# Unpacking 4-bit weights without the exclusive or, and a reordered opening, in a macaron block on one core

## The chip, the cores and the metric

The kernel runs on one NeuronCore of a Trainium2 chip. Its engines work side by side, each in the order of its own queue: TensorE (PE) multiplies and transposes into PSUM, VectorE (DVE) and ScalarE (ACT) work on SBUF and PSUM, GpSimd (POOL) on SBUF only, and SyncE (SP) starts most transfers. ACT and POOL start a few transfers too. Semaphores carry the waits between engines. The metric is the device time of one execution in microseconds (us), as the median of several runs.

## The reference

The input `u` has 2 x 1024 rows of 1024 values (2048 tokens). Three blocks are added to it in turn:

```python
x = x + 0.5 * ffn(layernorm(x))
x = x + s4(layernorm(x))          # a convolution along the last axis, by FFT, plus D * u
x = x + 0.5 * ffn(layernorm(x))

# ffn, with weights packed as 4-bit numbers, eight in a 32-bit word:
W[k, n] = scales[k // 128, n] * (w4[k, n] - (z4[k // 128, n] + 1))
h = silu(x @ Wg) * (x @ Wu)       # 1024 -> 2752
out = h @ Wd                      # 2752 -> 1024
```

Both feed-forward blocks use the same weights. `z4` are zero points, packed in the same way, one for each group of 128 rows.

## The kernel before

**Jobs.** The tokens are cut into four blocks of 512. Each block passes twice through the feed-forward part, so there are eight jobs (`JOBS`), and `fast()` writes them out one after the other. A job has a gate/up stage (`gate_up`, L650) and a down stage (`down`, L713). The gate/up stage has 48 steps: seven waves of column tiles (`WAVES`), each with eight groups of 128 input rows. A wave of three column tiles has six units (gate and up), held in six PSUM banks. In each step every unit gets two matmuls of 128x128 by 128x512, one with the low part and one with the high part of the activations. Then the unit's accumulator is multiplied by the ratio of two groups' scales: even units on ACT (L620), odd ones on DVE (L622). The next step's matmul on this bank waits for that. The down stage has 2 x 22 steps of four accumulators, in the same manner. The S4 block of a token block is worked in between the steps of the following job.

**Weights.** Nothing is stored unpacked at the start. In job 0 the packed words are loaded (`fetch`, L445), the zero points are loaded from a table in DRAM (`fetch_zeros`, L452, from `z_dram`, which `zero_points` writes at L305), and `signed_bytes` unpacks: a shift and mask for the even numbers (L459), one for the odd (L461), an addition of the zero-point table (L465), and an exclusive or with 0x8080 that turns biased bytes into signed ones (L467). All four are on DVE. `dequantize` (L499) copies every fourth byte of a row into a dense int8 tile `q` (pool of four buffers), on POOL, and SP writes it to DRAM (L503). From there each step's tile of int8 weights is loaded (`load_bytes`, L580, four steps ahead) and cast to fp32r three steps ahead (`make_weights`, L594 to L598): on POOL, but on ACT for three of eight steps in job 0. The down weights are unpacked in the same way (`dequantize_down`, L531), late in job 0's gate/up stage and during its down stage. All later jobs load the int8 weights.

**Order.** `at(hooks, s, f)` puts a piece of work ahead of step `s`. Engines' queues are filled by a planner that simulates the instructions with a cost of its own and takes, on each engine, the earliest written instruction that is ready in this simulation. `in_order_of_writing(f, engines)` binds what `f` writes to the written order on these engines, behind what was written before; what is written later is not bound to it.

**Opening.** `start()` (L1434) loads the packed zero points on ACT's queue, the rows of the first 512 tokens on SP's and ACT's, then packed words and scales. DVE unpacks the zero points, writes them to `z_dram`, and takes the moments of four row tiles (L186). Wave 0 is unpacked with zero points read back from `z_dram`. DVE and POOL share wave 0's eight byte copies; its first tile also goes directly from `q` into SBUF (L502, on POOL's queue), and DVE casts it (L594). ACT subtracts means (L1422), multiplies by inverse deviations (L1426), PE transposes, and ACT and DVE copy the result in two parts into `xT` (L246, L247). The second half of the columns follows in steps 0 to 3 (`second_half`).

Of the kernel before, what the change touches and what calls it, by code (L numbers as in the profile page):

```python
# [9 lines left out]
F32 = mybir.dt.float32  # L10
BF16 = mybir.dt.bfloat16
F16 = mybir.dt.float16
I32 = mybir.dt.int32
I8 = mybir.dt.int8
U16 = mybir.dt.uint16
F32R = mybir.dt.float32r
AF = mybir.ActivationFunctionType
# [6 lines left out]
P = 128  # L24
# [30 lines left out]
def macaron_s4_kernel(  # L55
# [116 lines left out]
    def rows_of(dram, b):  # L172
        return [dram[bass.ds(b * TB + t * P, P), :] for t in range(NT)]

    def moments(b, k, then=None):
        for _ in moments_by_tile(b, k, then):
            pass

    def moments_by_tile(b, k, then=None):

        name = f"{b}_{k}"
        stats = small.tile([P, NT, 2, 6], F32, tag="stats", name=f"stats_{name}")
        mv = small.tile([P, NT, 2], F32, tag="mv", name=f"mv_{name}")
        for t in range(NT):
            for i in range(2):
                nc.vector.bn_stats(stats[:, t, i, :], x[b][t][:, bass.ts(i, 512)])  # L186
            nc.vector.bn_aggr(mv[:, t, :], stats[:, t, :, :].rearrange("p a s -> p (a s)"))
            if then:
                then(t, mv[:, t, 0:1])
            yield  # L190
        ve = small.tile([P, NT], F32, tag="ve", name=f"ve_{name}")
        nc.vector.tensor_scalar(ve, mv[:, :, 1], EPS, None, ALU.add)
        r = small.tile([P, NT], F32, tag="r", name=f"r_{name}")
        half = small.tile([P, NT], I32, tag="half", name=f"half_{name}")
        nc.vector.tensor_scalar(half, ve.bitcast(I32), 1, None, ALU.logical_shift_right)
        nc.vector.tensor_scalar(
            r.bitcast(I32), half, -1.0, float(0x5F3759DF), ALU.mult, ALU.add
        )
        ln[b] = (mv, ve, r)
# [79 lines left out]
            nc.scalar.dma_start(z[own], src.rearrange("g (s n) -> (g s) n", s=SEG))  # L279
        return z  # L280

    def zero_points(which, z):

        p, n = z.shape
        zi = t2(f"zi_{which}").bitcast(I32)[:p, : 8 * n]
# [9 lines left out]
        tab = t2(f"ztab_{which}").bitcast(I32)[:p, : 8 * n]  # L295
        nc.vector.tensor_scalar(
            tab.bitcast(U16).rearrange("p (n k) -> p n k", k=2),
            zi.unsqueeze(2).to_broadcast([p, 8 * n, 2]),
            -8.0 * 257,
            120.0 * 257,  # L300
            ALU.mult,
            ALU.add,
        )
        dst, seg, queue = (zd_dram, SEGD, nc.sync) if which else (z_dram, SEG, nc.scalar)
        queue.dma_start(dst.rearrange("g (s n) -> (g s) n", s=seg), tab)  # L305

# [128 lines left out]


    first_tile = bpool.tile([P, width_of(0)], I8, tag="b", name="b_0_0")
    packed = {}
    NIBBLES = 0x78787878

# [14 lines left out]
    def signed_bytes(key, raw, even, z):  # L455

        nc.vector.tensor_scalar(even, raw, 3, NIBBLES, ALU.logical_shift_left, ALU.bitwise_and)  # L459
        yield  # L460
        nc.vector.tensor_scalar(raw, raw, 1, NIBBLES, ALU.logical_shift_right, ALU.bitwise_and)  # L461
        yield
        for part in (even, raw):
            both = part.bitcast(U16)
            nc.vector.tensor_tensor(both, both, z.bitcast(U16), ALU.add)  # L465
            yield
            nc.vector.tensor_scalar(both, both, 0x8080, None, ALU.bitwise_xor)  # L467
            yield
        view = lambda a: a.bitcast(I8).rearrange("p (n k) -> p k n", k=4)
        packed[key] = view(even), view(raw)  # L470

    def split(w):
        raw, z = packed[w]
        even = t4(f"even_{w}").bitcast(I32)[:, : width_of(w)]
        return signed_bytes(w, raw, even, z)

    def in_pieces(at, hooks_and_steps, pieces):

# [16 lines left out]
    def dequantize(w, j):  # L495

        q = qpool.tile([P, width_of(w)], I8, tag="q", name=f"q_{w}_{j}")
        engine = nc.vector if w == 0 and j % 3 < 2 else nc.gpsimd
        engine.tensor_copy(q, packed[w][j % 2][:, j // 2, :])  # L499
        dst = w_q[w].rearrange("(r j) n -> j r n", j=8)[j]  # L500
        if w == 0:
            nc.gpsimd.dma_start(first_tile[j:P:8], q[: P // 8])  # L502
        nc.sync.dma_start(dst, q)  # L503
        if j == 7:
            packed.pop(w)

# [15 lines left out]

    def split_down(a, rt):
        both, z = packed[a, rt]
        return signed_bytes((a, rt), both[:, 0], both[:, 1], z)

    def dequantize_down(a, rt, j):
        src = packed[a, rt][j % 2][:, j // 2, :]
        n = src.shape[0]
        q = qpool.tile([P, 512], I8, tag="q", name=f"qd_{a}_{rt}_{j}")[:n]  # L530
        nc.gpsimd.tensor_copy(q, src)  # L531
        rows = wd_q[a][8 * P * rt : 8 * P * rt + 8 * n]
        nc.sync.dma_start(rows.rearrange("(r j) n -> j r n", j=8)[j], q)
        if j == 7:
            packed.pop((a, rt))

    def first_weights(up, dn, at):


        for w in range(1, len(WAVES)):  # L540
            s0 = 8 * w - 12
            if w > 1:
                both = lambda w=w: (fetch(w), fetch_zeros(w))
                at(up, max(0, s0 - 5), lambda both=both: in_order_of_writing(both, ET.SP))
                steps = [(up, max(1, s0 - d)) for d in (3, 2, 2, 1, 1, 1)]
                in_pieces(at, steps, lambda w=w: split(w))
            else:
                both = lambda: [None for _ in split(1)]
                at(up, 0, lambda both=both: in_order_of_writing(both, *STARTING))
            for j in range(8):  # L550
                s = s0 + j if w > 1 else j // 2
                at(up, s, lambda w=w, j=j: dequantize(w, j))
        s0 = len(STEPS) - 12
        when = lambda n: (up, s0 + n) if n < 12 else (dn, (5 * (n - 12)) // 6)
        for n in range(6 * 8):
            k, j = divmod(n, 8)
            a, rt = divmod(k, 3)
            if j == 0:
                at(*when(max(0, n - 7)), lambda a=a, rt=rt: fetch_down(a, rt))
                steps = [when(max(0, n - d)) for d in (4, 3, 3, 2, 1, 0)]  # L560
                in_pieces(at, steps, lambda a=a, rt=rt: split_down(a, rt))
            at(*when(n), lambda a=a, rt=rt, j=j: dequantize_down(a, rt, j))

# [25 lines left out]
    def make_weights(i):  # L589
        j, stage, s = queue[i]  # L590
        b = loaded.pop(i)
        made[i] = t = wpool.tile(list(b.shape), F32R, tag="w", name=f"w_{stage}_{j}_{s}")
        if i == 0:
            nc.vector.tensor_copy(t, b)  # L594
        elif j == 0 and stage == "up" and s % GK in (1, 2, 5):
            nc.scalar.copy(t, b)
        else:
            nc.gpsimd.tensor_copy(t, b)  # L598
# [710 lines left out]
    def fast():  # L1309
        for j, (b, k) in enumerate(JOBS):  # L1310
# [50 lines left out]
            if j == 0:  # L1361
                rows = {3: srow_next}
                for s, k0, k1 in ((4, 3, 9), (16, 9, 15), (32, 15, WIDE)):
# [2 lines left out]
                        at(up, s - 5, load)  # L1366
                    at(up, s - 2, lambda k0=k0, k1=k1: scales(k0, k1, rows.pop(k0)))
                at(up, 40, scales_down)
                for t in range(NT):
                    at(up, t, lambda t=t: in_order_of_writing(lambda: second_half(t), *STARTING))  # L1370
                first_weights(up, dn, at)
# [59 lines left out]

    means = {}

    def start():  # L1434
        zeros = zero_words(0)
        x[0] = [t4(f"x_0_{t}") for t in range(NT)]
        for t, src in enumerate(rows_of(u, 0)):
            (nc.sync, nc.scalar)[t // 2].dma_start(x[0][t], src)
        fetch(0)
        srow = scale_rows(0, 3)  # L1440
        zeros_down = zero_words(1)
        fetch(1)
        rows_next = scale_rows(3, 9)
        zero_points(0, zeros)
        fetch_zeros(0)
        fetch_zeros(1)

        def then(t, m):
            means[t] = m
            less_mean(t, 0)  # L1450
            if t == 2:
                next(first_bytes)
                next(first_bytes)

        first_bytes = split(0)
        moments(0, 1, then)
        deviations(0, 1, -LIFT)
        for _ in first_bytes:
# [12 lines left out]
        return rows_next  # L1471

    srow_next = in_order_of_writing(start, *STARTING)
    x.pop(0)
    fast()
    x.clear()
# [85 lines left out]
```

## Time and profile before

| | |
|---|---|
| median of three runs | 2150.17 us (2148.67 to 2150.4) |
| profiled execution | 2152.6 us, of which the span 2150.7 |
| PE / DVE / ACT / POOL busy | 2092.5 / 1704.3 / 1422.3 / 1062.5 us |
| first gate/up matmul | 29.04 us |
| DMA, mean | 62 GB/s |

The profile is one execution on the chip. Busy time of an engine is the time in which at least one of its instructions ran; the ends of matmuls are modelled, so a busy PE isn't PE at its peak, and counting matmuls says more. A group's row gives line, engine, operation, result and operands, how many, and then busy time, mean ns of one, and the idle time just before with what ended it. The chain of waits is followed back from the last instruction, each time to what released it.

### The profile page before, as it was taken

How to read it: one execution, taken by the hardware profiler on the slowest of the kernel's cores; microseconds unless marked ns; L12 is line 12 of the kernel's file. 1: busy time of each engine (PE TensorE's matmuls, PEld its weight loads, DVE VectorE, ACT ScalarE, POOL GpSimd, SP SyncE). 2: the span in 40 equal slices, each digit the busy share in tenths (PEclk: the TensorE clock that was granted, in tenths of full speed). 3: DMA queues.
4: the chain of work that ended last, by engine and by line, in shares of the span. 5: the costliest groups of instructions: out<-in, count | busy, mean ns of one | idle time of the engine just before them, and what ended most of it. 6: DMA issues, size and time to landing. Idle time of an engine off the chain costs nothing.

```text
span 2150.7 us, 30258 instructions
## 1 busy us (share of the span) xinstructions
PE 2092.5 (97%) x9748; PEld 1425.5 (66%) x9748; DVE 1704.3 (79%) x2783; ACT 1422.3 (66%) x2233; POOL 1062.5 (49%) x1420
## 2 busy tenths in 40 slices
PE   4999999999999999999999999999999999999998
PEld 2555675577867568665776568676686766866576
DVE  7888978578788877778777788878788787777776
ACT  5887677646654776676767767646776467767765
POOL 3767747554344543455335553454534455345642
PEclk9999999999999999999999999999999999999999
DMA  4425232112111211212221121112111121121111
GB/s 136 116 85 148 78 92 59 32 54 76 41 41 54 89 53 39 78 33 58 87 80 36 31 74 37 38 52 77 35 36 41 52 93 48 44 81 36 34 35 57
DMA packets 163544, 132.49 MB, mean 62 GB/s; under 512 B 22252, under 2 KB 151029, under 8 KB 163376
## 3 DMA queue, kind: packets, MB, share of 16 engines
q1 hardware_dynamic: 162528, 129.12, 19.9%
q8 instruction: 79, 1.29, 0.3%
q10 hardware_dynamic: 592, 1.25, 0.2%
q14 instruction: 89, 0.73, 0.1%
q0 software_dynamic: 256, 0.10, 0.0%
HBM read 104.79 MB, written 25.50 MB: 61 GB/s over the span
## 4 chain that ended last, share of the span: by engine, by line
PE 87%; DVE 7%; POOL 2%; issue 1%; DMA 1%; ACT 1%; SPq 0%; DVEq 0%; ACTq 0%; POOLq 0%
PE pg L650 53%; PE po L713 27%; PE pc L1040 3%; DVE pg L622 2%; PE pb L735 1%; PE pb L1040 1%; PE pt L224 1%; DVE po L622 1%; PE st L224 1%; POOL w_down L598 0%; DVE hf L680 0%; POOL qd L531 0%; PE s_k L954 0%; DVE even L465 0%; ACT g L677 0%
## 5 line engine op out<-in xcount | busy, mean ns | idle before, releaser
L620 ACT ACTIVATE pg<-pg,rat 128x512 f32<-128x512 f32 x1240 | 787.3, 661 | 435.7 <-PE pg L650 434.8
L622 DVE TENSOR_TENSOR pg<-pg,rat 128x512 f32<-128x512 f32 x1168 | 776.1, 693 | 182.4 <-PE pg L650 178.4
L650 PE MATMUL pg<-xTh,w_up 128*128 128x512 f32 x2752 | 852.3, 438 | 6.3 <-DVE pg L622 4.5
L650 PE MATMUL pg<-xTl,w_up 128*128 128x512 f16 x2752 | 723.2, 383 | 13.6 <-DVE w_up L594 6.6
L650 PEld LDWEIGHTS pg<-xTh,w_up 128*128 128x128 f32 x2752 | 520.2, 189 | 185.2 <-DVE pg L622 18.3
L598 POOL CAST w_up<-b 128x768 fp32r<-128x768 int8 (+2 forms) x487 | 377.6, 781 | 529.6 <-PE pg L650 428.6
L713 PE MATMUL po<-hl,w_down 128*128 128x512 f32 x1344 | 538.8, 403 | 9.4 <-DVE po L622 7.3
L620 ACT ACTIVATE po<-po,ratd 128x512 f32<-128x512 f32 x660 | 431.0, 662 | 158.9 <-PE po L713 158.7
L713 PE MATMUL po<-hh,w_down 128*128 128x512 f32 x1344 | 522.4, 391 | 0.0
L622 DVE TENSOR_TENSOR po<-po,ratd 128x512 f32<-128x512 f32 x620 | 427.0, 697 | 96.6 <-PE po L713 92.6
L650 PEld LDWEIGHTS <-w_up 128*128 128x128 bf16 x2752 | 228.4, 99 | 335.3 <-issue 153.1
L598 POOL CAST w_down<-bd 128x512 fp32r<-128x512 int8 x352 | 222.5, 634 | 405.3 <-PE po L713 340.7
L713 PEld LDWEIGHTS po<-hl,w_down 128*128 128x128 f32 x1344 | 251.9, 188 | 86.2 <-DVE po L622 20.5
L713 PEld LDWEIGHTS po<-hh,w_down 128*128 128x128 f32 x1344 | 252.8, 188 | 45.2
L684 POOL TENSOR_TENSOR hl<-hf,hh 128x512 fp32r<-128x512 f32 x168 | 217.0, 1292 | 7.9
L680 DVE SCALAR_TENSOR_TENSOR hf<-pg,rat,g 128x512 f32<-128x512 f32 x168 | 122.9, 748 | 47.0 <-ACT g L677 37.4
L677 ACT ACTIVATE g<-pg,rat 128x512 f32<-128x512 f32 x168 | 110.6, 687 | 48.8 <-PE pg L650 38.9
L682 POOL CAST hh<-hf 128x512 fp32r<-128x512 f32 x168 | 106.4, 633 | 62.6 <-PE pg L650 30.5
L186 DVE BATCH_NORM_STATS2 stats<-x 128x6 f32<-128x512 f32 x96 | 63.6, 676 | 0.5
L1070 DVE TENSOR_TENSOR x<-x,pc 128x512 f32<-128x512 f32 x32 | 21.9, 685 | 36.9 <-PE pc L1040 36.9
L224 PE MATMUL pt<-ident,xn 128*128 128x128 f32 x256 | 43.2, 282 | 7.7 <-ACT xn L1426 7.7
L1040 PEld LDWEIGHTS pc<-near,st 128*128 128x128 f32 x256 | 43.6, 190 | 7.9
(177 smaller groups left out, 1043.3 us busy)
## 6 DMA issues: line engine op xcount, KB each, us to landing
b<-wq SPq DMA_DIRECT2D x319, 96.0 KB
bd<-wdq SPq DMA_DIRECT2D x336, 64.0 KB
x<-in_L_attn_u_dram SPq DMA_DIRECT2D x30, 512.0 KB
b<-wq SPq DMA_DIRECT2D x128, 64.0 KB
xs<-x SPq DMA_DIRECT2D x16, 512.0 KB
x<-xs SPq DMA_DIRECT2D x16, 512.0 KB
out_dram<-x SPq DMA_DIRECT2D x16, 512.0 KB
b<-wq SPq DMA_DIRECT2D x64, 80.0 KB
```

What stands on the lines that cost most here:

```text
L186: nc.vector.bn_stats(stats[:, t, i, :], x[b][t][:, bass.ts(i, 512)])
L224: nc.tensor.transpose(ps[:, bass.ts(k, P)], n[:, bass.ts(k, P)], ident)
L598: nc.gpsimd.tensor_copy(t, b)
L620: nc.scalar.activation(dst, src, AF.Copy, scale=sc)
L622: nc.vector.tensor_tensor(dst, src, sc.to_broadcast([P, TB]), ALU.mult)
L650: nc.tensor.matmul(p, weights, (lo, hi)[k][:, g, :], start=(g == 0 and not done), stop=(g == GK - 1 and done), skip_group_check=True,)
L677: nc.scalar.activation(g, pg, AF.Silu, scale=rat[:, 2 * f, GK - 1 :])
L680: nc.vector.scalar_tensor_tensor(hf, pu, last, g, ALU.mult, ALU.mult)
L682: nc.gpsimd.tensor_copy(hi, hf)
L684: nc.gpsimd.tensor_tensor(lo, hf, hi.bitcast(F32), ALU.subtract)
L713: nc.tensor.matmul(ps[c], w[:, bass.ts(c, P)], part, start=(f == 0 and k == 0), stop=(f == NF - 1), skip_group_check=True,)
L1040: nc.tensor.matmul(dst, lhsT, rhs, start=start, stop=stop, skip_group_check=True)
```

## The change

There are three parts.

- Unpacking leaves the bytes biased by 128 (`biased_bytes`): the exclusive or is gone, two of six DVE operations for each wave and each piece of the down weights. The byte copy now subtracts 128 from an unsigned byte (`to_signed`), on POOL, for two tiles of wave 0 on ACT. Since there are fewer operations, the pieces are placed otherwise: a wave's four operations come together one step ahead of its first copies, a down piece's four in four successive places; a wave is fetched three steps ahead instead of five.
- In the opening, the packed words of wave 0 and its packed zero points come first, the rows after them. The zero points of wave 0 are spread over their rows by the load itself (`first_zero_words`) and unpacked in place (`first_zeros`), so wave 0 no longer reads `z_dram`. DVE unpacks and POOL and ACT copy bytes before the moments are taken. ACT takes the moments of row tile 1 (a mean by accumulation, then squares of the differences), DVE those of the other three. `zero_points(0)` comes at the end of the opening, that of the down weights at step 12, and the second halves' mean subtractions (for three tiles) after `zero_points(0)`. The first tile's transfers move from POOL's queue to SP's. The first three casts are on POOL. An activation with Silu at the start loads ACT's table.
- `keep_warm` gives PE transposes whose result nobody reads: 12 before the first turn, one after each turn, six after the last. PE, too, is now bound to the written order in the opening.

The diff (without the renaming of callers and the import of `U8`):

```diff
@@ def moments_by_tile(b, k):
             nc.vector.bn_aggr(mv[:, t, :], stats[:, t, :, :].rearrange("p a s -> p (a s)"))
-            if then:
-                then(t, mv[:, t, 0:1])
             yield
+        guess(b, k, mv)
+
+    def guess(b, k, mv):
...
+    def unpacked_zeros(tab, z, zi):
...
+    def zero_points(which, z):
+        p, n = z.shape
+        zi, tab = (t2(f"{a}_{which}").bitcast(I32)[:p, : 8 * n] for a in ("zi", "ztab"))
+        unpacked_zeros(tab, z, zi)
         dst, seg, queue = (zd_dram, SEGD, nc.sync) if which else (z_dram, SEG, nc.scalar)
...
+    def first_zero_words():
+        n = width_of(0) // 8
+        z = t2("zq_first").bitcast(I32)[:, :n]
+        for own, i, lo, hi in columns(0):
+            own = slice(own.start // 8, own.stop // 8)
+            src = (gate_qz, up_qz)[i][:, lo // 8 : hi // 8]
+            wide = src.unsqueeze(1).to_broadcast([GK, 16, own.stop - own.start])
+            nc.scalar.dma_start(z[:, own], wide)
+        return z
+
+    def first_zeros(zq):
+        n = width_of(0)
+        z, zi = (t4(f"{a}_w0").bitcast(I32)[:, :n] for a in ("z", "zi"))
+        unpacked_zeros(z, zq, zi)
+        packed[0][1] = z
...
             nc.vector.tensor_tensor(both, both, z.bitcast(U16), ALU.add)
             yield
-            nc.vector.tensor_scalar(both, both, 0x8080, None, ALU.bitwise_xor)
-            yield
-        view = lambda a: a.bitcast(I8).rearrange("p (n k) -> p k n", k=4)
+        view = lambda a: a.bitcast(U8).rearrange("p (n k) -> p k n", k=4)
...
+    def to_signed(q, part, on_act=False):
+        if on_act:
+            nc.scalar.activation(q, part, AF.Identity, bias=minus_128)
+        else:
+            nc.gpsimd.tensor_scalar(q, part, -128.0, None, ALU.add)
...
-        engine = nc.vector if w == 0 and j % 3 < 2 else nc.gpsimd
-        engine.tensor_copy(q, packed[w][j % 2][:, j // 2, :])
+        to_signed(q, packed[w][j % 2][:, j // 2, :], on_act=w == 0 and j in (0, 2))
         if w == 0:
-            nc.gpsimd.dma_start(first_tile[j:P:8], q[: P // 8])
+            nc.sync.dma_start(first_tile[j:P:8], q[: P // 8])
...
-                at(up, max(0, s0 - 5), lambda both=both: in_order_of_writing(both, ET.SP))
-                steps = [(up, max(1, s0 - d)) for d in (3, 2, 2, 1, 1, 1)]
-                in_pieces(at, steps, lambda w=w: split(w))
+                at(up, s0 - 3, lambda both=both: in_order_of_writing(both, ET.SP))
+                in_pieces(at, [(up, s0 - 1)], lambda w=w: split(w))
...
-                steps = [when(max(0, n - d)) for d in (4, 3, 3, 2, 1, 0)]
+                steps = [when(max(0, n - d)) for d in (3, 2, 1, 0)]
...
-        if i == 0:
-            nc.vector.tensor_copy(t, b)
-        elif j == 0 and stage == "up" and s % GK in (1, 2, 5):
+        if j == 0 and stage == "up" and s > 2 and s % GK in (1, 2, 5):
             nc.scalar.copy(t, b)
...
+                zeros = lambda: zero_points(1, zeros_down)
+                at(up, 12, lambda: in_order_of_writing(zeros, ET.DVE, ET.SP))
...
+    def first_moments():
+        stats = small.tile([P, NT, 2, 6], F32, tag="stats", name="stats_0_1")
+        mv = small.tile([P, NT, 2], F32, tag="mv", name="mv_0_1")
+        own = 1
+        means.update({t: mv[:, t, 0:1] for t in range(NT)})
+        scratch = t4("scratch")
+        nc.scalar.activation(
+            scratch, x[0][own], AF.Copy, scale=1.0 / HID, accum_out=means[own]
+        )
+        for half in range(2):
+            less_mean(own, half)
+        squares = small.tile([P, 2], F32, tag="squares", name="squares")
+        for half in range(2):
+            nc.scalar.activation(
+                scratch[:, bass.ts(half, 512)], first[own, half], AF.Square,
+                scale=HID**-0.5, accum_out=squares[:, half : half + 1],
+            )
+        for t in (0, 2, 3):
+            for i in range(2):
+                nc.vector.bn_stats(stats[:, t, i, :], x[0][t][:, bass.ts(i, 512)])
+            nc.vector.bn_aggr(mv[:, t, :], stats[:, t, :, :].rearrange("p a s -> p (a s)"))
+            less_mean(t, 0)
+        nc.vector.tensor_tensor(mv[:, own, 1:2], squares[:, 0:1], squares[:, 1:2], ALU.add)
+        guess(0, 1, mv)
+
+    def keep_warm(n, src=None):
+        ps = bank("warm")
+        for k in range(n):
+            nc.tensor.transpose(ps[:, :P], ident if src is None else src[:, :P], ident)
+
     def start():
-        zeros = zero_words(0)
+        zq = first_zero_words()
+        fetch(0)
         x[0] = [t4(f"x_0_{t}") for t in range(NT)]
         for t, src in enumerate(rows_of(u, 0)):
-            (nc.sync, nc.scalar)[t // 2].dma_start(x[0][t], src)
-        fetch(0)
+            (nc.sync, nc.scalar)[t % 2].dma_start(x[0][t], src)
+        nc.gpsimd.memset(minus_128, -128.0)
+        warm = small.tile([P, 1], F32, tag="warm", name="warm")
+        nc.scalar.activation(warm, minus_128, AF.Silu)
         srow = scale_rows(0, 3)
+        zeros = zero_words(0)
         zeros_down = zero_words(1)
+        first_zeros(zq)
+        for _ in split(0):
+            pass
+        for j in (0, 2, 4, 6, 1, 3, 5, 7):
+            dequantize(0, j)
         fetch(1)
         rows_next = scale_rows(3, 9)
-        zero_points(0, zeros)
-        fetch_zeros(0)
-        fetch_zeros(1)
-
-        def then(t, m):
-            means[t] = m
-            less_mean(t, 0)
-            if t == 2:
-                next(first_bytes)
-                next(first_bytes)
-
-        first_bytes = split(0)
-        moments(0, 1, then)
+        first_moments()
+        keep_warm(12, first[NT - 1, 0])
         deviations(0, 1, -LIFT)
-        for _ in first_bytes:
-            pass
-        for i in range(8):
-            dequantize(0, i)
         for t in range(NT + 1):
             if t < NT:
                 by_deviation(t, 0)
             if t:
                 turn(0, t - 1, first[t - 1, 0], 0)
-        for t in range(NT):
+                keep_warm(6 if t == NT else 1)
+        scales(0, 3, srow)
+        zero_points(0, zeros)
+        fetch_zeros(1)
+        for t in (0, 2, 3):
             less_mean(t, 1)
-        scales(0, 3, srow)
-        zero_points(1, zeros_down)
-        return rows_next
+        return rows_next, zeros_down
 
-    srow_next = in_order_of_writing(start, *STARTING)
+    srow_next, zeros_down = in_order_of_writing(start, *STARTING, ET.PE)
```

More of the change, by code (lines that the diff above doesn't have):

```diff
@@ L14 @@
 I8 = mybir.dt.int8
+U8 = mybir.dt.uint8
 U16 = mybir.dt.uint16
@@ L173, in rows_of, with moments, moments_by_tile @@
         return [dram[bass.ds(b * TB + t * P, P), :] for t in range(NT)]
-    def moments(b, k, then=None):
-        for _ in moments_by_tile(b, k, then):
+    def moments(b, k):
+        for _ in moments_by_tile(b, k):
             pass
-    def moments_by_tile(b, k, then=None):
+    def moments_by_tile(b, k):
         name = f"{b}_{k}"
@@ L187, in moments_by_tile @@
             nc.vector.bn_aggr(mv[:, t, :], stats[:, t, :, :].rearrange("p a s -> p (a s)"))
-            if then:
-                then(t, mv[:, t, 0:1])
             yield
+        guess(b, k, mv)
+    def guess(b, k, mv):
+        name = f"{b}_{k}"
         ve = small.tile([P, NT], F32, tag="ve", name=f"ve_{name}")
@@ L280, in zero_words @@
         return z
-    def zero_points(which, z):
+    def unpacked_zeros(tab, z, zi):
         p, n = z.shape
-        zi = t2(f"zi_{which}").bitcast(I32)[:p, : 8 * n]
         for k in range(8):
@@ L294, in zero_points @@
             )
-        tab = t2(f"ztab_{which}").bitcast(I32)[:p, : 8 * n]
         nc.vector.tensor_scalar(
@@ L437, in macaron_s4_kernel @@
     first_tile = bpool.tile([P, width_of(0)], I8, tag="b", name="b_0_0")
+    minus_128 = const.tile([P, 1], F32, tag="minus_128", name="minus_128")
     packed = {}
@@ L453, in fetch_zeros, with biased_bytes @@
         packed[w][1] = z
-    def signed_bytes(key, raw, even, z):
+    def first_zero_words():
[12 more added lines that the diff above has]
+        packed[0][1] = z
+    def biased_bytes(key, raw, even, z):
         nc.vector.tensor_scalar(even, raw, 3, NIBBLES, ALU.logical_shift_left, ALU.bitwise_and)
@@ L474, in split @@
         even = t4(f"even_{w}").bitcast(I32)[:, : width_of(w)]
-        return signed_bytes(w, raw, even, z)
+        return biased_bytes(w, raw, even, z)
     def in_pieces(at, hooks_and_steps, pieces):
@@ L497, in dequantize @@
         q = qpool.tile([P, width_of(w)], I8, tag="q", name=f"q_{w}_{j}")
-        engine = nc.vector if w == 0 and j % 3 < 2 else nc.gpsimd
-        engine.tensor_copy(q, packed[w][j % 2][:, j // 2, :])
-        dst = w_q[w].rearrange("(r j) n -> j r n", j=8)[j]
+        to_signed(q, packed[w][j % 2][:, j // 2, :], on_act=w == 0 and j in (0, 2))
         if w == 0:
-            nc.gpsimd.dma_start(first_tile[j:P:8], q[: P // 8])
-        nc.sync.dma_start(dst, q)
+            nc.sync.dma_start(first_tile[j:P:8], q[: P // 8])
+        nc.sync.dma_start(w_q[w].rearrange("(r j) n -> j r n", j=8)[j], q)
         if j == 7:
@@ L524, in split_down @@
         both, z = packed[a, rt]
-        return signed_bytes((a, rt), both[:, 0], both[:, 1], z)
+        return biased_bytes((a, rt), both[:, 0], both[:, 1], z)
     def dequantize_down(a, rt, j):
@@ L530, in dequantize_down @@
         q = qpool.tile([P, 512], I8, tag="q", name=f"qd_{a}_{rt}_{j}")[:n]
-        nc.gpsimd.tensor_copy(q, src)
+        to_signed(q, src)
         rows = wd_q[a][8 * P * rt : 8 * P * rt + 8 * n]
@@ L1432, in macaron_s4_kernel @@
     means = {}
+    def first_moments():
[12 more added lines that the diff above has]
+            nc.scalar.activation(
+                scratch[:, bass.ts(half, 512)],
+                first[own, half],
+                AF.Square,
+                scale=HID**-0.5,
+                accum_out=squares[:, half : half + 1],
+            )
[6 more added lines that the diff above has]
+        guess(0, 1, mv)
```

## The prediction

> **What bounds the kernel.** I read the page first: engine shares, then slices.
>
> ```profile
> PE 2092.5 (97%) x9748; PEld 1425.5 (66%) x9748; DVE 1704.3 (79%) x2783; ACT 1422.3 (66%) x2233; POOL 1062.5 (49%) x1420
> ...
> PE   4999999999999999999999999999999999999998
> ...
> POOL 3767747554344543455335553454534455345642
> ```
>
> TensorE (PE) sets the end; only the first slices have holes. The stage table of busy times puts numbers on them (columns: stage, its length, then PE, PEld, DVE, ACT, POOL; below, the gate/up matmuls of L650 alone: PE, PEld).
>
> ```profile
> 29.00:62.00 33.00, 27.91 (x110) 15.33 (x111) 26.11 (x54) 22.33 (x37) 18.97 (x22) 0.90 0.41 116
> 62.00:212.00 150.00, 144.25 (x634) 83.40 (x633) 127.92 (x199) 118.36 (x189) 108.85 (x135) 1.00 0.39 113
> 210.00:250.00 40.00, 35.67 (x146) 23.61 (x145) 38.44 (x71) 28.37 (x47) 28.72 (x40) 1.00 0.22 63
> 240.00:280.00 40.00, 37.10 (x169) 27.80 (x168) 32.79 (x44) 27.71 (x47) 39.50 (x54) 1.00 0.38 116
> ...
> 29.00:62.00 33.00, 26.33 (x88) 13.19 (x89) 0.90 0.41 116
> 62.00:212.00 150.00, 140.36 (x602) 79.72 (x600) 1.00 0.39 113
> ```
>
> In a late job twelve L650 matmuls start every 2.70 us (timeline: groups of six begin at 1989.63 and 1992.33), 0.225 us each. So 88 matmuls are 19.8 us and, with 16 transposes at about 0.11, fill 21.6 of the 33 us: 11 us lost. In 62 to 212 the 602 (and 11 of L713) are 138 us: 12 lost. Job 0 runs from 29 to about 307, 278 us; a job without the S4 work takes 245 (865 to 1110). So 29 us of opening and 33 us of loss can be won; the other seven jobs don't contain what is changed. The chain of waits names the early losses:
>
> ```profile
> 1.33 4.88 DMA zq<-in_L_ffn_up_qzeros_dram
> ...
> 22.39 2.06 DMA b<-q
> ...
> 28.42 0.57 DVE w_up L594
> ...
> 43.17 4.83 DMA z<-z_dram
> 48.09 0.96 DVE even L465
> 49.05 0.62 DVE pg L622
> 49.71 19.41 PE pg L650 x71
> ```
>
> The start hangs on packed zeros, then on the first bytes and their cast. The second stall hangs on wave 2's zero points: DVE waits for them with a scaling of the accumulators queued behind, and PE stands 3.94 us. From 50.30 to 56.16 PE issues 14 matmuls, 3.15 us' worth: 2.7 us more, at a granted clock of 0.50 and then 0.77.
>
> [...]7 matmuls take 3.11 us from 29.04[...]. [...]POOL's 128x768 copy takes 1.49 us under the exclusive ors and adds, 0.83 otherwise.[...]
>
> **The change, part by part.**
>
> *Opening.* Packed zeros of wave 0 come broadcast straight from DRAM instead of through `z_dram`; rows are loaded after raw words. Before, the zero words landed at 6.27; they are again first on ACT's queue, so I keep 6.3. DVE then: eight unpacks over 96 instead of 43 columns (0.105 us before; 0.16 by the extra columns) 1.3; table of 1536 elements (688 took 0.52, 512 took 0.42) 1.0; two shifts 1.1; first add 0.95. The even bytes stand at 10.7, the odd at 11.6. ACT makes two q tiles, 10.7 to 12.5; POOL makes six at 0.83, one at 1.49. There are four q buffers, so the fifth waits until the first one's two writes have landed: its SP issues end near 12.5, +2.0 (the old first-tile DMA's landing) is 14.5. Four copies follow to 17.8, a last DMA of 2.4 to 20.2, POOL's cast 0.85: first weights at 21. The first-tile DMAs move from POOL's queue to SP's: 16 issues at about 0.4 us, with wave 1's raw words and the next scales behind them; these are needed after 30.
>
> The rows are later than the weights. ACT, behind its q tiles: mean over 1024 1.3, two subtractions 1.3, two squares with accumulation 1.7: to 16.8; three more subtractions to 18.8. DVE's three tiles of moments (1.46 each) end at 16.0; it waits for the squares, then guess and Newton steps, 2.55 before: 19.5. From there to the last copied quarter took 6.0 us before (16.98 to 23.1), but the 12 warming transposes stand in PE's order ahead of the first turn: they start at 18.8 and, at about 0.22 each[...] (estimate: eight took 1.97 from 17.85, latency included), end at 21.4, 1.2 us after the first turn is ready. With the last subtraction (0.68) the first matmul comes at 19.5+5.5+1.2 = 26.2 against 29.04: **-2.8**. Bounds 24 and 28.5. If transposes hold the clock, 3.11-1.57 is saved at the start: **-1.5** (0 if they don't, the one way in which the change wouldn't do what it says). The first casts move to POOL, idle then: nothing; without the cover 0.85 each. The Silu table load moves from 61.95 to the idle start: PE had no gap at 61.95, so nothing.
>
> *29 to 62.* The wait for wave 2's zeros can go, since its fetch and split move later relative to each other (fetch at step 1, one split at step 3). At stake are 3.94+2.7 = 6.6. But wave 1's zero points are now later: `zero_points(0)` stands at the end of the start, so z_dram is written near 31.5 (before: 12), the broadcast lands near 34 to 36, and wave 1's split ends near 38, where it ended at 40.3 before; behind it queue POOL's eight conversions, their writes on SP, wave 2's fetch, and the loads for step 8. Also ACT issues the z_dram write and then three subtractions (2.0 us, before in the idle time at 23) ahead of the second halves. Wave 1's first weights therefore can't come before about 52, and PE reaches step 8 there instead of at about 62 only if nothing else waits. I take half of the stall: **-3.3** (0 to -6.6).
>
> *Exclusive or gone.* Rows of before:
>
> ```profile
> L467 DVE TENSOR_SCALAR rawd<-rawd 128x1024 uint16<-128x1024 uint16 x8 | 5.2, 650 | 0.0
> ...
> L467 DVE TENSOR_SCALAR raw<-raw 128x1536 uint16<-128x1536 uint16 x5 | 3.4, 674 | 0.0
> L467 DVE TENSOR_SCALAR even<-even 128x1536 uint16<-128x1536 uint16 x5 | 3.2, 635 | 0.0
> ```
>
> All 28 are about 17 us, of which some 12.6 fall after 62, where PE waits for DVE's scalings for 20.7 us by the waits table (weight loads included). DVE is at 38.4 of 40 us in 210 to 250, so time off it counts there; elsewhere it has room. I count a third: **-4** (0 to -9).
>
> *Against it.* A wave's split was three groups of at most three operations; now four in a row, 3.0 us. DVE's slack per accumulator is about 1.1 us (1.8 from its last matmul to the next use, less 0.69), so the group stalls PE about 1.8 once a wave where the groups of two and three cost about 1.3 together: 0.5 for six waves[...]. `zero_points(1)`, 1.26 us of DVE hidden ahead of the first scaling, now falls into step 12: 0.5. Together **+2** (0 to +5).
>
> *GpSimd subtracts.* Nearest rows: a copy of 128x384 takes 0.512 and of 128x128 0.296, and the selecting operation of the same size 0.293. An operation with arithmetic thus ran at the copy's rate[...]. I take +0.03 per tile, **+1**[...].
>
> Sum: -2.8-1.5-3.3-4+2+1 = -8.6. The profiled execution took 2152.6 us, 1.9 of it outside the span of 2150.7; it would go to 2144.0. The median of runs, 2150.17, lies 2.4 below that execution: 2141.6.
>
> **The ways it can go.**
>
> 1. As summed, 2136 to 2146, forecast 2141.6; chance 0.53.
> 2. Everything at stake comes back: stall 6.6, DVE 9, no new clumps: -2.8-1.5-6.6-9+1 = -18.9, 2131. For it: DVE's near-full stage. Against: 240 to 280 is POOL's, 39.5 of 40. Chance 0.17.
> 3. A new wait replaces the old: wave 1's zero points hold step 8 until 60, so opening and stall give nothing; -4+2+1 leaves 2149. For it: that write moves 20 us; against: old wave 1 wasn't early either. Chance 0.19.
> 4. Slower: the subtraction runs at the upper price. In 240 to 280 POOL handles 21 down tiles[...]; of the other 28, half[...]; in the up waves [...]a POOL slack of 4.0 a wave (21.6 less 4.2 of casts, 7.5 of copies, 5.9 of hidden units)[...]. From about +0.3 us on a 512-column tile it loses. [...]against: the selecting row. Chance 0.11.
>
> No change that a measurement could tell is 0.2%, 4.3 us. Faster is 1 and 2, 0.70; the same 0.19; slower 0.11. The range runs from 2129 (just under case 2) to 2152 (beyond 3); 4 and a little below are left out.
>
> **What would show it.** First L650 matmul at 24 to 28.5, and full rate at once; ACT's first scaling within 2 us of PE's first finished accumulator (if the z_dram write blocks ACT's queue, it comes at 30 or later and the opening's gain is gone); no PE wait of 3 us before step 8, whose gate activation ran at 63.24; POOL's 128x768 form at 0.83 to 0.90 (1.2 and more is case 4); DVE's waits by PE after 62 below 17 us; jobs 1 to 7 unchanged within 2 us in all. The weakest step is wave 1's zero points: a first wait of PE at step 8 on POOL's casts would make case 3 true.

## The result: slower by 57 us, all of it in job 0

The changed kernel takes 2207.61 us (median of 4 runs, 2206.32 to 2209.26) against 2150.28, a ratio of 1.0269 with a 95% interval of 1.0251 to 1.0286. The forecast was 2141.6 with a range of 2129 to 2152. The profiled execution took 2207.78 us, of which the span 2205.9.

The last down matmul of job 0 starts at 305.3 us before and at 362.8 after, 57.5 later; the first one starts at 209.2 before and at 236.8 after. So job 0 lost 27.6 up to the end of its gate/up stage and 29.9 in its down stage. What follows takes as long in both profiled executions but for 2.3 us (1845.4 before, 1843.1 after), so jobs 1 to 7 lost nothing.

The page of the kernel after, engine shares and slices:

```profile
PE 2114.0 (96%) x9769; PEld 1439.9 (65%) x9769; DVE 1693.8 (77%) x2755; ACT 1424.2 (65%) x2239; POOL 1171.6 (53%) x1420
...
PE   5888879999999999999999999999999999999998
...
POOL 6999993854335453355534553354533446345542
PEclk9899989999999999999999999999999999999999
```

Before, PE had nines from the second slice on. Now slices 2 to 6 (each 55 us) have eights and a seven, and in the same slices POOL has nines where it had 7, 6, 7, 7 and 4. POOL is busy 109 us longer with as many instructions (1420). Whoever sees only the shares, 49% before and 53% after, sees a harmless engine.

The stage table of the kernel after (stage, length, then busy time and number of instructions of PE, PEld, DVE, ACT and POOL, then granted clock, DMA share and GB/s):

```profile
62.00:100.00 38.00, 31.42 (x118) 17.57 (x116) 27.53 (x46) 21.12 (x34) 37.92 (x26) 0.85 0.33 95
100.00:150.00 50.00, 44.28 (x198) 25.80 (x197) 39.72 (x59) 36.09 (x58) 49.59 (x37) 1.00 0.29 85
...
280.00:330.00 50.00, 37.90 (x146) 28.75 (x145) 23.32 (x35) 26.28 (x43) 49.83 (x48) 0.86 0.29 90
```

POOL is full: 37.92 of 38 us, 49.59 of 50, 49.83 of 50. Its groups by form say with what:

```profile
L500 POOL TENSOR_SCALAR qd<-rawd 128x512 int8<-128x512 uint8 x32 | 49.5, 1560 | 0.3 <-POOL qd L500 0.3
L500 POOL TENSOR_SCALAR q<-raw 128x768 int8<-128x768 uint8 x20 | 42.6, 2133 | 0.0
L500 POOL TENSOR_SCALAR q<-even 128x768 int8<-128x768 uint8 x18 | 40.1, 2231 | 11.2 <-DVE even L490 11.2
```

The copies in their place took 699, 830 and 1051 ns, by the same view of before:

```profile
L531 POOL COPY qd<-rawd 128x512 int8<-128x512 int8 x32 | 21.8, 699 | 6.9 <-DMA wdq<-qd 3.8 <-issue 1.1 <-DVE e L208 1.1
...
L499 POOL COPY q<-even 128x768 int8<-128x768 int8 x17 | 17.9, 1051 | 25.3 <-DVE even L467 21.0 <-DMA wq<-q 3.8 <-POOL q L499 0.5
L499 POOL COPY q<-raw 128x768 int8<-128x768 int8 x17 | 14.1, 830 | 1.6 <-DVE raw L467 1.0 <-DMA b<-q 0.6
```

With all shapes the subtractions take 194.2 us, the copies of before 80.3. (There are eight waves and 64 steps in a gate/up stage, not seven and 48 as described above: POOL converts 62 tiles of them, and 48 of the down weights.)

How a long tile on POOL becomes a hole in PE is to be seen twice. In the down stage it is direct. The waits of 236 to 364 us:

```profile
PEld po L738 <- POOL w_down L623: 29.2, 11, 4.3
PE po L738 <- POOL w_down L623: 24.3, 10, 3.9
```

Before, the same waits (209 to 306 us) were short:

```profile
PEld po L713 <- POOL w_down L598: 2.2, 3, 0.7
...
PE po L713 <- POOL w_down L598: 0.3, 1, 0.3
```

One of the long ones, each line a start, a duration, engine and instruction:

```profile
243.68 3.43 POOL L500 TENSOR_SCALAR qd<-rawd 128x512 int8<-128x512 uint8 x2
...
247.06 0.60 POOL L623 CAST w_down<-bd 128x512 fp32r<-128x512 int8 x1
...
247.72 0.79 PE L738 MATMUL po<-hl,w_down 128*128 128x512 f32 x1 [3.77 <-POOL w_down L623]
```

Two subtractions of 1.7 us stand on POOL ahead of a cast of down weights, and PE waits 3.77 us for that cast. In all PE stands 24.0 us longer for these casts than before, most of the 29.9 that the stage lost. Matmuls behind such a hole are slow as well: after this one they start 0.43 us apart until 250.5, where 0.225 is the rate of a late job. How much of the remaining 6 us that makes was not counted. In the gate/up stage POOL shows in two ways. The waits of PE from 28 to 237 us:

```profile
PE pg L675 <- DVE pg L647: 14.6, 6, 5.2
PE pg L675 <- POOL w_up L623: 10.0, 7, 2.8
PE ps_d L362 <- DMA drow<-n_L_ffn_down_scales_dram: 4.7, 1, 4.7
```

Before (28 to 209 us) the first was 9.0 and the second 1.8, and the third did not occur. The second is the direct way again, a cast of weights behind subtractions; the third, a load on SP's queue, was not followed further. The first takes more steps. The timeline around 50 us:

```profile
47.33 4.51 SPq L531 DMA_DIRECT2D wq<-q  x3
...
49.36 2.12 POOL L500 TENSOR_SCALAR q<-raw 128x768 int8<-128x768 uint8 x1
...
51.46 2.12 POOL L500 TENSOR_SCALAR q<-even 128x768 int8<-128x768 uint8 x1
51.88 0.42 SPq L453 DMA_DIRECT2D raw<-_L_ffn_gate_qweight_dram  x1
...
54.22 1.81 SPq L531 DMA_DIRECT2D wq<-q  x2
54.98 1.10 DVE L484 TENSOR_SCALAR even<-raw 128x768 int32<-128x768 int32 x1 [8.04 <-DMA raw<-in_L_ffn_up_qweight_dram]
```

SP's queue holds the writes of `q` and, behind them, the fetch of wave 2's packed words. The writes come at POOL's pace of 2.1 us, so the fetch is issued at 51.88, DVE stands 8.04 us for its words with scalings of accumulators behind them in its order, and PE stands 5.2 us for a scaling. (With copies in place of the subtractions, the first experiment below, the fetch is issued at 46.33 and DVE stands 1.1 us.) The granted clock drops too: 0.73 in 45 to 62, where it was 0.80 before.

### The profile page after: what moved, and what is told of

It is laid out like the page before. It is cut to its first block, busy times and chain, and to the rows that moved or that the text cites. A ratio compares the mean times of both kernels' runs of the same rounds, so it can differ in the third digit from the quotient of the medians.

```text
span 2205.9 us, 30276 instructions
## 1 busy us (share of the span) xinstructions
PE 2114.0 (96%) x9769; PEld 1439.9 (65%) x9769; DVE 1693.8 (77%) x2755; ACT 1424.2 (65%) x2239; POOL 1171.6 (53%) x1420
## 4 chain that ended last, share of the span: by engine, by line
PE 81%; DVE 3%; ACT 0%; issue 0%; DVEq 0%; ACTq 0%
PE pg L675 48%; PE po L738 25%; PE pc L1065 3%; PE pb L760 1%; PE pb L1065 1%; DVE pg L647 1%; PE pt L227 1%; PE st L227 1%; DVE po L647 0%; DVE hf L705 0%; PE s_k L979 0%; ACT g L702 0%; DVE hb L721 0%; DVE hf_half L719 0%; DVE r L212 0%
## 5 line engine op out<-in xcount | busy, mean ns | idle before, releaser
L675 PE MATMUL pg<-xTh,w_up 128*128 128x512 f32 x2752 | 856.7, 439 | 17.9 <-DVE pg L647 14.6
L675 PE MATMUL pg<-xTl,w_up 128*128 128x512 f16 x2752 | 725.7, 384 | 10.8 <-POOL w_up L623 9.2
L675 PEld LDWEIGHTS pg<-xTh,w_up 128*128 128x128 f32 x2752 | 521.9, 190 | 193.8 <-DVE pg L647 30.1
L738 PE MATMUL po<-hl,w_down 128*128 128x512 f32 x1344 | 545.8, 408 | 27.8 <-POOL w_down L623 24.3
L738 PE MATMUL po<-hh,w_down 128*128 128x512 f32 x1344 | 528.7, 396 | 0.0
L675 PEld LDWEIGHTS <-w_up 128*128 128x128 bf16 x2752 | 228.4, 99 | 339.0 <-issue 154.6
L500 POOL TENSOR_SCALAR qd<-rawd 128x512 int8<-128x512 uint8 (+1 forms) x48 | 73.3, 1541 | 0.3 <-POOL qd L500 0.3
L500 POOL TENSOR_SCALAR q<-even 128x768 int8<-128x768 uint8 (+2 forms) x30 | 59.2, 1976 | 11.2 <-DVE even L490 11.2
L500 POOL TENSOR_SCALAR q<-raw 128x768 int8<-128x768 uint8 (+2 forms) x32 | 61.7, 1930 | 0.0
L187 DVE BATCH_NORM_STATS2 stats<-x 128x6 f32<-128x512 f32 x88 | 58.5, 676 | 0.5
```

The costliest lines, as they stand in the source:

```text
L500: nc.gpsimd.tensor_scalar(q, part, -128.0, None, ALU.add)
L675: nc.tensor.matmul(p, weights, (lo, hi)[k][:, g, :], start=(g == 0 and not done), stop=(g == GK - 1 and done), skip_group_check=True,)
L738: nc.tensor.matmul(ps[c], w[:, bass.ts(c, P)], part, start=(f == 0 and k == 0), stop=(f == NF - 1), skip_group_check=True,)
```

## The experiments

Theory A in the first experiments: the price of GpSimd's subtraction is the loss. From "The change with two operations" on it is narrower: the price is that of the instruction with a single operation. Ratios are to the kernel before as it was timed beside each group of runs (2151.20, 2150.60 and 2150.34 us). In the diffs "-" is the kernel before or after that is named, "+" the experiment.

**The change without its subtraction.** From the kernel after; the subtraction is left out, so the bytes that GpSimd copies stay off by 128.

```diff
-            nc.gpsimd.tensor_scalar(q, part, -128.0, None, ALU.add)
+            nc.gpsimd.tensor_copy(q, part.bitcast(I8))
```

> The changed kernel, but GpSimd copies the bytes as before instead of subtracting 128 (the subtraction is left out on GpSimd, so its bytes stay biased; the two tiles on ACT still subtract). Theory A, the price of the subtraction is the whole loss: 2136 to 2148 us, with GpSimd's 128x768 form back at about 0.83 us. Theory B, half or more of the loss comes from the late zero points of wave 1, the four operations in a row and PE's bound order: 2175 us or more, with PE waits on DVE's scalings before 60 us as in the changed kernel.

2144.45 us (2142.74 to 2146.53), ratio to before 0.997 (0.996 to 0.998). The last down matmul of job 0 starts at 297.5. All 57 us are gone with this line, and 6 more.

**The subtraction's instruction alone.** From the kernel before; its copies in waves 1 to 7 and of the down weights become an addition of zero.

```diff
-        nc.gpsimd.tensor_copy(q, src)
+        nc.gpsimd.tensor_scalar(q, src, 0.0, None, ALU.add)
```

> The kernel before with one thing of the change: GpSimd's copies become an addition of 0 to the signed byte (waves 1 to 6 and the down weights; wave 0 as before), everything else, the exclusive or too, stays. Theory A: 2190 to 2215 us, GpSimd's forms at about 1.5 us for 512 and 2.1 us for 768 columns. Theory B: 2170 us or less.

2205.74 us, ratio 1.0252 (1.0235 to 1.0269): this form of instruction, with nothing else of the change, gives a loss of 54.5 us, nearly that of the whole change.

**The opening alone.** From the kernel before: the new opening with its warming transposes and `zero_points(1)` at step 12; exclusive or, copies (two of wave 0's on ACT) and placement of the later waves as before.

> The changed kernel with the packing of before: exclusive or on DVE, plain byte copies on GpSimd (and on ACT for the two tiles of wave 0), pieces and fetches placed as before; the new opening stays. Theory A: 2140 to 2151 us, as the opening itself is worth 0 to 8 us. Theory B: 2160 us or more, as wave 1's zero points are late here too.

2153.27 us, ratio 1.001 (1.0004 to 1.0017). The opening is worth nothing, or costs some 2 us.

**What an operation costs on GpSimd.** A kernel that only runs each form four times; the block's computation is left out. The other engines are idle, except that DVE and ACT run a form of their own until 7.4 us.

> Not the computation of the reference: a program that only runs GpSimd operations on 128 partitions, four of each form back to back with all other engines idle, and copies the input to the output. It measures the price by itself. If arithmetic is what costs (any addition of a constant, whatever the types and the stride): about 2.1 us for every 768-column addition, float to float and dense too, against 0.83 for the copies. If byte operands or the stride of 4 bytes cost: the dense float addition near 0.85 to 1.3 us and only the byte forms at 2.1.

Groups by form (mean ns of one is the number ahead of the second bar):

```profile
L113 POOL TENSOR_SCALAR d<-words 128x768 int8<-128x768 uint8 x4 | 9.1, 2276 | 0.0
L116 POOL TENSOR_SCALAR d<-words 128x768 int8<-128x768 int8 x4 | 8.5, 2125 | 0.0
L119 POOL TENSOR_SCALAR d<-words 128x768 int8<-128x768 uint8 x4 | 8.5, 2125 | 0.0
L125 POOL TENSOR_SCALAR d<-fsrc 128x768 f32<-128x768 f32 x4 | 8.5, 2122 | 0.0
L131 POOL TENSOR_SCALAR d<-fsrc 128x512 f32<-128x512 f32 x4 | 5.9, 1484 | 0.0
L137 POOL TENSOR_TENSOR d<-fsrc 128x768 f32<-128x768 f32 x4 | 5.8, 1458 | 0.0
...
L122 POOL COPY d<-words 128x768 int8<-128x768 int8 x4 | 3.3, 818 | 0.0
...
L134 POOL TENSOR_SCALAR d<-fsrc 128x128 f32<-128x128 f32 x4 | 2.1, 522 | 0.0
```

L113 is the form of the change, every fourth byte; its mean holds a first one of 2.73 us, and the other three took 2.12. L116 adds 0 to every fourth byte, L119 takes dense bytes, L125 f32. So type and stride don't matter here: 2.12 to 2.13 us in all four. From 128 to 768 columns it is (2122-522)/640 = 2.5 ns per column, plus 0.2 us. Adding a constant is dearer than adding a tensor to itself (1458), or taking one tensor from another (1797 in the second kernel of forms below). DVE does the byte subtraction in 0.810.

**Without the exclusive or.** From the kernel before, L467 taken out (left out: the bytes stay biased), the pieces where they were.

```diff
-            nc.vector.tensor_scalar(both, both, 0x8080, None, ALU.bitwise_xor)
-            yield
```

> The kernel before with the exclusive or left out (so its bytes stay biased) and nothing else changed: opening, placement and GpSimd's copies are those of before. It measures what VectorE's 28 operations are worth. If the 9 us between the two earlier runs (opening with copies and no exclusive or, 2144.5; opening with exclusive or, 2153.3) are the exclusive or's: 2140 to 2144 us, and PE's waits for DVE's scalings after 62 us fall. If they are the placement's or the opening's: 2147 to 2152 us.

2144.86 us, ratio 0.9973 (0.9962 to 0.9983).

**And with the new placement.** As the last one (the exclusive or left out), with the changed kernel's fetch and piece positions.

```diff
-                at(up, max(0, s0 - 5), lambda both=both: in_order_of_writing(both, ET.SP))
-                steps = [(up, max(1, s0 - d)) for d in (3, 2, 2, 1, 1, 1)]
+                at(up, s0 - 3, lambda both=both: in_order_of_writing(both, ET.SP))
+                in_pieces(at, [(up, s0 - 1)], lambda w=w: split(w))
...
-                steps = [when(max(0, n - d)) for d in (4, 3, 3, 2, 1, 0)]
+                steps = [when(max(0, n - d)) for d in (3, 2, 1, 0)]
```

> As the run without the exclusive or (left out here too), with the changed kernel's placement of the pieces (four in a row one step ahead, fetch three steps ahead). My prediction put the placement at +2 us (0 to +5): 2 us above the run without the exclusive or. If the later fetch makes DVE wait for zero points, 6 us or more above it.

2139.61 us, ratio 0.995 (0.9934 to 0.9967): the placement gains 5 us more. The waits of 40 to 62 us name the stall, in the kernel before, then without the exclusive or, then with the placement as well:

```profile
PE pg L650 <- DVE pg L622: 4.2, 2, 3.9
```

```profile
PE pg L648 <- DVE pg L620: 4.6, 2, 3.8
```

```profile
PE pg L647 <- DVE pg L619: 0.8, 2, 0.5
```

**No warming.** The first experiment without `keep_warm`'s transposes (its subtraction left out as there).

> The run with the changed kernel and plain copies on GpSimd (subtraction left out, 2144.5 us), without the transposes that keep PE busy. Theory W, they hold the clock: the first matmuls take 0.4 us each for about 3 us and the time rises by 1 to 2 us. Theory Q, they only stand in the way of the turns: the first matmul comes about 1 us sooner and the time is the same or lower.

2144.12 us against 2144.45, no difference. The first matmul of L675's kind comes at 28.06, and at about full rate: 12 of them start in 3.03 us, where the first seven took 3.11 before. So it is not the warming transposes that give this rate. Before, PE had stood 6.55 us ahead of its first matmul; here the transposes that the opening needs anyway end 0.48 us ahead of it. Whether the shorter pause is what counts, no run sets apart.

**One operation or two.** Again forms alone, the block left out: a column as constant, and an instruction with two operations, add -128 and multiply by 1.0.

> Not the computation of the reference: GpSimd operations alone again, four of each form, all other engines idle but for one form on ACT. A constant given as a column in SBUF, and two operations in one instruction. If a constant in the instruction is the slow part, the column form is near 0.85 us; [...]both are at 2.1 us or more. ACT's identity with a bias column should be near 0.9 us for 768 columns.

```profile
L119 POOL TENSOR_SCALAR d<-words,col 128x768 int8<-128x768 uint8 x4 | 8.8, 2205 | 0.1
...
L122 POOL TENSOR_SCALAR d<-words 128x768 int8<-128x768 uint8 x4 | 3.3, 829 | 0.0
L116 POOL COPY d<-words 128x768 int8<-128x768 int8 x4 | 3.3, 822 | 1.9 <-DMA words<-_L_ffn_gate_qweight_dram 1.9
```

With a second operation that does nothing, the subtraction runs at the copy's rate: 829 against 822 ns.

**The change with two operations.** From the kernel after:

```diff
-            nc.gpsimd.tensor_scalar(q, part, -128.0, None, ALU.add)
+            nc.gpsimd.tensor_scalar(q, part, -128.0, 1.0, ALU.add, ALU.mult)
```

> The changed kernel with one more operation in GpSimd's instruction: add -128, then multiply by 1.0. Theory A (what costs is the instruction with a single operation, not the subtraction): q tiles at 0.83 to 1.05 us for 768 columns, and 2144.5, as the run that copied without subtracting (2144.45). Theory B (the subtraction itself is dear beside DVE's work, and the short time was only that of an idle chip): tiles over 1.5 us, and 2165 to 2208.

2145.58 us (2142.69 to 2146.53), ratio 0.9974 (0.9966 to 0.9983). Its groups on POOL:

```profile
L500 POOL TENSOR_SCALAR qd<-rawd 128x512 int8<-128x512 uint8 x32 | 21.1, 673 | 4.3 <-DVE rawd L490 2.5 <-issue 1.1 <-DMA bd<-wdq 0.6
L500 POOL TENSOR_SCALAR q<-even 128x768 int8<-128x768 uint8 x18 | 18.3, 1021 | 16.6 <-DVE even L490 16.6
```

673 and 1021 ns, where the copies took 699 and 1051. Theory A in its narrow form holds: what costs is the instruction with a single operation, not the subtraction, also beside DVE's work.

**The old opening with the rest of the change.** From the kernel before: biased bytes, the subtraction with two operations on POOL, the new placement. DVE's six tiles of wave 0 subtract with `nc.vector.tensor_scalar`.

> The kernel before with only the first part of the change, the subtraction in the form with two operations (in wave 0 DVE's five tiles subtract with one operation, 0.81 us by the row measured alone). Theory A: 2139.5 to 2142, the run without the exclusive or and with the new placement (2139.61) and nothing for the subtraction, below both kernels. Theory B: over 2160.

2140.41 us (2138.03 to 2142.98), ratio 0.9952 (0.9935 to 0.9969): 10 us below the kernel before and 67 below the changed one.

**The new opening without the unpacking at step 12.** From the changed kernel with two operations:

```diff
-                zeros = lambda: zero_points(1, zeros_down)
-                at(up, 12, lambda: in_order_of_writing(zeros, ET.DVE, ET.SP))
...
+        zero_points(1, zeros_down)
         return rows_next, zeros_down
```

> As the first kernel of this group, but the down weights' zero points are unpacked at the end of the opening again, and not at step 12. Theory C (the opening's gain is eaten by that unpacking, 2.8 us of DVE ahead of PE's scalings[...]): 2140 to 2142 against 2144.5. Theory D (it is wave 1's late zero points and the late ratios that eat it): 2144 to 2147, as the unpacking only moves into the stretch where ACT and DVE are late anyway.

2140.59 us, ratio 0.9957 (0.9941 to 0.9974), 5 us below 2145.58. Theory C: this one step ate 5 us. The chain of waits of the run with copies shows how, each line a start, a duration and what ran:

```profile
71.77 1.50 DVE raw L490
73.26 1.21 DVE pg L647 x2
74.47 2.82 DVE zi L289 x8
77.29 0.60 DVE pg L647
77.93 1.01 PE pg L675 x3
```

The eight unpacks of the down weights' zero points come close behind a wave's unpacking, with scalings of accumulators behind them in DVE's order. (One takes 0.18 to 0.84 us there in the run with two operations, and 0.18 to 0.19 in the opening of this one; POOL copies beside them at step 12, but no run shows what stretches them.) PE stands 1.90 us and is slow after that: six matmuls from 81.40 take 2.08 us, where six of a late job take 1.74. Counted in gate/up matmuls of 62 to 80 us, first with step 12, then without:

```profile
62.00:80.00 18.00, 15.29 (x65) 8.21 (x63) 0.98 0.50 141
```

```profile
62.00:80.00 18.00, 17.32 (x76) 9.72 (x75) 1.00 0.55 149
```

Eleven matmuls at 0.225 are 2.5 us in this stretch; from 80 to 100 it is 82 against 87, 1.1 us.

**Which placement.** From the kernel before without the exclusive or: only the waves' part of the placement.

> The kernel before without the exclusive or (left out, so the bytes stay biased), and of the new placement only the waves' part: fetch three steps ahead, the unpacking in one piece; the down pieces are placed as before. Theory E (the gain of the placement, 5.3 us, lies in wave 2's fetch and unpacking, where the kernel before stalled for 3.94 us): 2139 to 2141. Rival F (it lies in the down pieces, whose four operations come closer to their use): 2144 to 2145, as without the placement (2144.86).

2139.94 us, ratio 0.9951 (0.9934 to 0.9968), as with both parts (2139.61). Theory E: the gain lies in the waves. The down pieces' positions give nothing that shows.

## Why the prediction was wrong

**The step that failed: "GpSimd subtracts".** This term of the sum was put at +1 and measured 62 to 63 us: 2207.61 against 2145.58 with two operations and 2144.45 with copies. I took +0.03 us per tile because the selecting operation of 128x128 (0.293) ran at the copy's rate (0.296); that an addition of a constant would do so too, no row of before shows. Measured: +0.86 us per 512 columns (1.560 against 0.699) and +1.2 to +1.3 per 768, +113 us of POOL in all (194.2 against 81.0 in the run that copies). The row of a selecting instruction said nothing about this one: at its own size, 128x128, the addition takes 0.522 (L134 above). With two operations the subtraction takes 829 ns at 768 columns, close to the copy (818 to 822) and to DVE's subtraction (810); with one it takes 2.12 us, 2.5 ns for each column.

**Case 4 was the right mechanism at too low a price.** It named the place, POOL in 240 to 280 and a slack of 4.0 us a wave, and the point, +0.3 us on a 512-column tile. But its upper price was no bound: no trace or run had shown it. With the measured price, 0.86 us per 512 columns and 1.3 per 768, its own counts give, for seven waves of 1.3x8-4.0 = 6.4 us, about 45 (some 36 if the three narrower ones are counted by their widths), and for the down tiles, 21 and half of 28 as it counted, 35x0.86 = 30; 27.6 and 29.9 were lost. So the working, to which I gave a chance of 0.11, would have forecast a loss of 66 to 75 us, too large in the gate/up stage; that the 30 fits so well is in part luck, as half of the 28 was a guess. What spoke for it in the rows of before was work with two inputs: 474 against the copy's 296 ns at 128x128, 1194 against 512 at 128x384, 1.6 and 2.3 times as long.

**Opening, -2.8 and -1.5.** First matmul 26.2 forecast, 28.52 measured (27.93 with copies):

```profile
28.52 0.73 PE L675 MATMUL pg<-xTh,w_up 128*128 128x512 f32 x2 [0.87 <-POOL w_up L623]
```

"I keep 6.3" for the packed zeros was wrong: the broadcast load landed at 8.48 (in the chain 6.51 us against 4.88 before). The full rate from the start came true (nine matmuls start from 28.52 to 30.68), but not through the warming transposes: the run without them has it too. Both together gave nothing in the end (2153.27 against 2151.20 alone). With step 12 out of the way the new opening equals the old one (2140.59 and 2140.41): it has 48 gate/up matmuls done by 45 us against 44, and 104 against 105 by 62. In the run with copies PE waits 2.6 us in 45 to 48, in three waits, for a byte copy (1.03), for DVE's scaling (1.06) and for DVE's low part of the activations (0.46). ACT's first scaling comes at 30.82, after 3.1 us for the ratios that DVE now computes late: the sign that I had named for a lost gain, but not by the write that I had blamed. Wave 1's additions start at 40.46, where the run with the old opening and the same placement had them at 35.93. That is the weakest step that I had named, wave 1's late zero points, and case 3 in part; how much of it is due to the zero points and how much to the late ratios was not separated.

**29 to 62, -3.3, and placement, +2.** The stall did go, as half expected. But the placement removed it, not the opening: without the exclusive or and with the old opening it goes (longest wait 3.8 us, then 0.7) through the waves' placement alone, -4.9 us. I had put the stall under its own heading and then charged four operations in a row as a cost. They gain instead. Before, DVE waited 1.42 us for the table with a scaling behind it; with the placement it waits 0.63, and a scaling runs just ahead (46.51). That this order is the reason is read from the two traces and was not tested by itself. That `zero_points(1)` costs 0.5 at step 12 was ten times too little: 1.26 us of unpacking became 2.8, at the worst place, and cost 5.

**Exclusive or, -4.** A ratio of 0.9973 is -5.8, within the range of 0 to -9. After 62 PE waits for DVE's scalings 18.5 us where it was 21.1 before (to 340 us), so less than the fall below 17 that I had named.

**Sum.** Without the price of the subtraction my terms gave 2140.6; the run with copies took 2144.45. That this is near is luck: the opening, its unpacking at step 12 included, was taken at about -4 and gave +2, while stall and placement, taken together at -1.3, gave -5, and the exclusive or -5.8 for -4. The 4 us left over are about what the unpacking at step 12 costs. Jobs 1 to 7 were unchanged within 2.3 us, about as predicted.

## What to carry to other kernels

Before an instruction is moved to another engine or given another operation there, time that very form, with its number of operations and its width; a row of a neighbouring operation is no bound (at 128x128 the selection took 0.293 us, the addition 0.522). A share of 49% busy hides stages in which an engine has 4 us of slack in 20: price a change on it by the stage. And a small piece of work that is taken out of an idle stretch needs a new place as idle: 1.3 us set between scalings cost 5.

## What the runs showed of the hardware

GpSimd's tensor_scalar with one operation takes 2.12 us for 128x768, with a second, empty operation 0.83: adding a multiplication by 1.0 makes it 2.6 times faster. With a column in place of an immediate constant it is 2.21, also slow. Neither type nor stride changes this (2.12 to 2.13 us for bytes at a stride of four, dense bytes and f32). The single operation was an addition in every run; others were not timed. Why the form with one operation is slow no run shows.
